# Moving the steps of a weight folding within the first image's attention, and converting five more score tiles by DMA

## The chip, the cores and the metric

The kernel runs on one core of a Trainium2 chip. A core has a matrix engine (TensorE, PE in the profile), a vector engine (VectorE, DVE), a scalar engine (ScalarE, ACT), a general engine (GpSimd, POOL) and an engine that mostly issues DMAs (SyncE, SP). Each engine works through its own list of instructions in order, and engines wait for each other through semaphores. The metric is the device time of one execution in microseconds (us), as the median of several runs. Lower is better.

## The reference, cut to what matters

Two layers are applied to a tensor of 8 images, 512 channels and 32 x 32 pixels. Each is a normalisation, an attention over the 1024 pixels and a projection with a residual. The first has 8 heads of 64 channels and rounds q, k and v to 8 bits; the second has one head of 512 channels.

```
# layer 0
h = group_norm(x)
q, k, v = split(qkv_w @ h + qkv_b)            # 8 heads of 64 channels
q, k, v = fake_quant(q), fake_quant(k), fake_quant(v)
w = softmax(q*s . k*s)                        # over 1024 keys
x = x + proj_w @ (w . v) + proj_b
# layer 1
t = group_norm(x)
q, k, v = t @ wq.T + bq, t @ wk.T + bk, t @ wv.T + bv
x = x + (softmax(q . k / sqrt(512)) . v) @ wp.T + bp
```

For layer 1 the kernel needs only two products of weights, wq with wk and wv with wp. It forms them once. This is the folding, whose steps the change moves.

## The kernel before

The kernel has three stages: q, k and v of all images, with the ranges for the rounding; the first image's attention in layer 0; then, for each image, its projection and layer 1, into which the attention of the next image is woven.

**Units of attention.** The attention of layer 0 is cut into units, numbered by u through all images. A unit is one pair of heads (j), one half of the 1024 queries (hf) and one of eight blocks of 128 keys (s). So u % 8 is s, and an image has 64 units: units 0 to 63 are the first image's, and unit 64 is the second's first. For each unit:

- `scores(u)` forms both heads' scores on PE in a PSUM tile st, and ACT writes their exponential (exp) as 32-bit floats. There are two such PSUM tiles. The scores of unit u + 2 wait until the exponential of unit u has been taken.
- `split(u)` turns the exponential (pt) into two 16-bit parts in the tile two: a copy of it in float16, and what the copy lost, which DVE subtracts (`rest`). Who makes the copy depends on the image and on s. In the first image a DMA issued by GpSimd makes it for s in `CAST_BY_DMA` (0, 1, 4), DVE for s = 6, and ACT for s = 2 and 5. Units with s = 3 and 7 are used as 32-bit floats (the tile aside), without a copy. In later images there are no such plain units: GpSimd copies s = 2 and 6, DVE copies s = 5 while the order is still the first image's, and ACT copies the others. A copy by DMA reads from one of three slots in a buffer called spare, not from a pt tile, and its subtraction is put off (`put_off`) to the third split after it or to when the parts are needed.
- `over_keys` multiplies the parts with v (av), and `totals` sums them (sm), both on PE, two units at a time. After the eighth key block `finish` has ACT copy av and sm out (to ao, and to rs or kept_u). The sums go through DRAM to be inverted and spread (`spread`), and DVE multiplies (`divide`).

In the loop the scores run six to nine units ahead of over_keys.

**Pairs.** `load_pair` loads the raw q, k and v of the next pair through SP's queue, and DVE rounds them (raw, q, k, v). In the first image's order these small works, with `spread` and `divide`, stand in a list `dealt`. Each call of split takes one that is due.

**Folding.** `fold()` is a generator. Each `next` carries out one step up to the next yield. For each of two products there are 16 steps of one 128x512 product on PE (fold), and every fourth is followed by an ACT copy (to wa or wm). A step with wt_f multiplies a widened vector that DVE must have written (into the first part of spare, from four reductions called z); ACT copies its result to fold_room. The next step, wc_f, multiplies fold_room by a constant. After the first product the generator also puts four additions (wa) in the list dealt and issues the loads of the projection weights and of the first image's input (`load_x2`, tile h, two DMAs of 1 MB). That input takes the place of the weights that wt_f reads last. At its end it puts four additions (wm) and two kinds of stores in the list. In all there are 35 yields. Nine steps are taken before the attention starts, the others inside `scores`, where the chosen units take one ahead of their products. Whatever is left runs when the first image's last unit is done.

**Order.** A helper class `InOrder` records the order of the instructions of PE, DVE and ACT (line 91 for DVE and ACT, line 209 for PE in the profile). While the first image's attention is recorded, its order is as written. Afterwards a planner with estimated costs orders the work of the later images. Its clock is set to PE's when planning begins, after two more groups of four units (`LEAD = 2`), so units up to 77 are scored and split in the order as written.

The lines that decide about the steps and the copies:

```
CAST_BY_DMA, CAST_BY_DVE = (0, 1, 4), (6,)
...
                if u % 8 in (1, 4, 6):
                    next(folding, None)
...
                elif b == 0 and s in CAST_BY_DMA:
                    at = (u // NT * len(CAST_BY_DMA) + CAST_BY_DMA.index(s)) % 3
...
                if b == 0 and s in CAST_BY_DMA:
                    nc.gpsimd.dma_start(two[:, 0], pt)
                    put_off[u] = rest
                    return
```

Of the kernel before, what the change touches and what calls it, by code (L numbers as in the profile page):

```python
# [22 lines left out]
NT = T // P  # L23
NH = T // 512
HEADS = 8
PAIRS = HEADS // 2
# [32 lines left out]
def attn_pair_kernel(  # L59
# [12 lines left out]
    class InOrder:  # L72
# [74 lines left out]
        def settle(self, what):  # L147

            while True:
                i = next((i for i, c in enumerate(self.chores) if c[0] == what), None)  # L150
                if i is None:
                    return
                self.begin(i)
# [3 lines left out]
    def elements(n):  # L157

        return 0.21 + n * 0.957e-3
# [4 lines left out]
    def awaits(t):  # L164

        pe.t = max(pe.t, t + 0.1)
# [41 lines left out]
    def mm(ps, lhsT, rhs, **kw):  # L208
        ins = nc.tensor.matmul(ps, lhsT=lhsT, rhs=rhs, **kw).ins  # L209
        part = lhsT.shape[-1] / P if lhsT.shape[-1] in (32, 64) else 1.0  # L210
        if rhs.dtype in (BF, F16, F32R):
            part *= 0.25 * lhsT.shape[0] / P
        pe.t += math.prod(rhs.shape[1:]) * 1.677e-3 * part
        if last_mm[0] is not None:
            tc.add_manual_dep(ins, last_mm[0].name, IN_ORDER, reason="order")
        last_mm[0] = ins
# [90 lines left out]
    with ExitStack() as fast:  # L307
        wts = fast.enter_context(tc.tile_pool(name="wts", bufs=1))
        def pair_ps(name):
            return ps_s.tile([P, 2, 512], F32, tag="s", name=name)  # L310
# [602 lines left out]
        def plain(b, s):  # L913
            return b == 0 and s % 4 == 3
# [4 lines left out]
        def deal(u):  # L919
            i = next((i for i, (at, *_) in enumerate(dealt) if at <= u), None)  # L920
            if i is not None:
                dealt.pop(i)[2]()
                if dealt[i : i + 1] and dealt[i][2].__name__ == "fetch_v":
                    dealt.pop(i)[2]()
# [7 lines left out]
            dve.settle(what)  # L932

        ao = {}
        CAST_BY_DMA, CAST_BY_DVE = (0, 1, 4), (6,)

        def load_pair(b, j, u=None):

# [54 lines left out]
        def attention():  # L993
# [13 lines left out]
            def scores(u):  # L1007
                b, j, hf, s = units[u]
                if hf == 0 and s == 0:
                    settle("qk")  # L1010
                nm = f"{b}_{j}_{hf}"
                qt, kt, _ = pairs[b, j]
                st = pair_ps(f"st_{nm}_{s}")
                if u % 8 in (1, 4, 6):
                    next(folding, None)
                awaits(st_free[-2])
                for i, r in enumerate(HALF):
                    mm(
                        st[:, i, :], lhsT=kt[r, bass.ts(s, P)],
                        rhs=qt[r, bass.ts(hf, 512)], start=True, stop=True,  # L1020
                    )
                if u >= 4:
                    need(u - 4)
                if plain(b, s):
                    pt = aside[:, u // 4 % 3].rearrange("p (i k) n -> p i (k n)", i=2)
                elif b == 0 and s in CAST_BY_DMA:
                    at = (u // NT * len(CAST_BY_DMA) + CAST_BY_DMA.index(s)) % 3
                    pt = spare[:, 1 + 2 * at : 3 + 2 * at].rearrange("p i k n -> p i (k n)")
                else:
                    pt = ptp.tile([P, 2, 512], F32, tag="p", name=f"pt_{nm}_{s}")  # L1030
                there = act.do(
                    1.12, lambda: act.activation(pt, st, AF.Exp, scale=esc),
                    max(pe.t + 0.25, ready.get(u - 4, 0.0) + 0.1),
                )
                st_free.append(there)
                pts[u] = pt, there

            def split(u):

                b, j, hf, s = units[u]  # L1040
                pt, there = pts.pop(u)
                if not InOrder.planned:
                    for v in [v for v in put_off if v < u - 2]:
                        put_off.pop(v)()
                    deal(u)
                if plain(b, s):
                    parts[u], ready[u] = pt, there
                    return
                two = partp.tile([P, 2, 2, 512], F16, tag="two", name=f"two_{b}_{j}_{hf}_{s}")
                parts[u] = two  # L1050

                def rest():
                    dve.tensor_tensor(two[:, 1], pt, two[:, 0], ALU.subtract)
                    ready[u] = dve.t

                if b == 0 and s in CAST_BY_DMA:
                    nc.gpsimd.dma_start(two[:, 0], pt)
                    put_off[u] = rest
                    return

                def cast(copy=act.copy):
                    at_hand.add(u)
                    copy(two[:, 0], pt)  # L1063
                    done_at = act.t if copy == act.copy else there + 1.5
                    dve.later("sum", elements(1024), rest, done_at + 0.1, 9.0)

                if b == 0:
                    cast(dve.tensor_copy if s in CAST_BY_DVE else act.copy)
                elif s % 4 == 2:
                    cast(nc.gpsimd.tensor_copy)  # L1070
                elif not InOrder.planned and s == 5:
                    cast(dve.tensor_copy)
                else:
                    act.later("cast", 1.02, cast, there, 7.0)

            def need(u):

                if u in put_off:
                    put_off.pop(u)()
                while u not in ready:  # L1080
                    e, name = (act, "cast") if u not in at_hand else (dve, "sum")
                    e.begin(next(i for i, c in enumerate(e.chores) if c[0] == name))
# [95 lines left out]
            for u in (0, 2, 4):  # L1178
                for i in (u, u + 1):
                    scores(i)  # L1180
                    split(i)
                yield 0
            for u in range(0, len(units), 4):
                b, j, hf, s = units[u]
# [15 lines left out]
                if not late:  # L1200
                    two(scores, u + 6)
                if late:
                    over_keys((u, u + 1))
                    two(scores, u + 6)
                    totals((u, u + 1))
                    over_keys((u + 2, u + 3))
                    totals((u + 2, u + 3))
                    two(split, u + 6)
                    two(scores, u + 8)
                elif dense:  # L1210
                    over_keys((u, u + 1))
                    totals((u, u + 1))
                    two(split, u + 6)
                    two(scores, u + 8)
                    over_keys((u + 2, u + 3))
                    totals((u + 2, u + 3))
                else:
                    over_keys(range(u, u + 4))
                    totals(range(u, u + 4))
                    two(split, u + 6)  # L1220
                    two(scores, u + 8)
# [1011 lines left out]
```

## Time and profile before

| | us |
|---|---|
| median of 3 runs | 2589.24 (2586.92 to 2589.48) |
| the profiled execution | 2589.42 |
| its span, first to last instruction | 2587.6 |

| Engine | busy us | share of the span |
|---|---|---|
| PE | 2524.7 | 98% |
| DVE | 1896.7 | 73% |
| ACT | 1352.1 | 52% |
| POOL | 183.7 | 7% |

The shares are means over the stages. In the stretch that the change touches ACT and DVE are far busier than over the whole:

| Stretch, us | length | PE | DVE | ACT | DMA share |
|---|---|---|---|---|---|
| 586 to 600 | 14 | 10.41 | 9.64 | 12.76 | 0.58 |
| 600 to 616 | 16 | 16.00 | 15.03 | 14.40 | 0.57 |
| 616 to 640 | 24 | 21.63 | 17.41 | 19.12 | 0.86 |
| 640 to 664 | 24 | 23.62 | 23.28 | 22.13 | 0.50 |
| 664 to 690 | 26 | 25.54 | 21.88 | 23.57 | 0.73 |
| 690 to 716 | 26 | 21.40 | 23.36 | 25.45 | 0.32 |

A matmul's end is modelled in the profile, so that a PE that reads as full may still be waiting in small gaps. In the lines of the profile an entry begins with its start and duration in us, then the engine, the line, the operation, and what is written from what. The number in square brackets is how long the engine was idle before it, and what ended that. A "x2" at the end of an entry means that two such instructions were merged.

### The profile page before, as it was taken

To read this page: it belongs to the slowest core of one execution; us is meant where nothing else is said; L and a number is where in the kernel's file an instruction comes from. 1 tells how busy PE (TensorE), PEld (TensorE's weight loads), DVE (VectorE), ACT (ScalarE), POOL (GpSimd) and SP (SyncE) were. 2 spreads that over 40 slices of the span, in tenths; PEclk is the share of its full clock that TensorE was granted. 3 is DMA by queue.
4 is the path that set the end of the run, shared out by engine and by line. 5 is a ranking of instruction groups with operands and counts; after the bars stand their busy time and mean duration, and the time that the engine had idled before them with its cause. 6 is when DMAs were issued, how large, how long until landed. Compare 5 with 4: busy or idle time off the path is not lost.

```text
span 2587.6 us, 38715 instructions
## 1 busy us (share of the span) xinstructions
PE 2524.7 (98%) x15670; PEld 1748.4 (68%) x15670; DVE 1896.7 (73%) x2748; ACT 1352.1 (52%) x1688; POOL 183.7 (7%) x161
## 2 busy tenths in 40 slices
PE   7999999999979999999999999999999999999998
PEld 4788888872237766775677577657756775777787
DVE  6788777658867777777877787777777777775544
ACT  3222222218946665665666466747665665664121
POOL 0000000001100001000100010010001000100000
PEclk9999999999989999999999999999999999999999
DMA  4343333337521232223212321232232123212211
GB/s 167 134 150 135 119 117 117 128 127 183 138 85 46 73 112 90 62 78 115 86 55 86 113 94 58 95 118 65 73 111 94 46 79 123 85 52 82 86 38 39
DMA packets 159469, 249.38 MB, mean 96 GB/s; under 512 B 26928, under 2 KB 93488, under 8 KB 157744
## 3 DMA queue, kind: packets, MB, share of 16 engines
q1 hardware_dynamic: 125264, 182.81, 21.3%
q10 hardware_dynamic: 30560, 57.71, 6.6%
q0 software_dynamic: 3456, 6.29, 1.3%
q8 instruction: 125, 2.05, 0.3%
q14 instruction: 64, 0.52, 0.1%
HBM read 153.64 MB, written 86.28 MB: 93 GB/s over the span
## 4 chain that ended last, share of the span: by engine, by line
PE 85%; DVE 4%; issue 3%; ACT 2%; DMA 1%; POOL 0%; SPq 0%; ACTq 0%; DVEq 0%; POOLq 0%
PE s L209 15%; PE o L209 14%; PE qkps L209 12%; PE pj L209 8%; PE av L209 8%; PE v2ps L209 7%; PE g L209 7%; PE vps L209 6%; PE st L209 4%; PE sm L209 3%; DVE two L91 1%; ACT pt L91 1%; DMA two<-spare 1%; DVE acc L91 1%; DVE h L91 0%
## 5 line engine op out<-in xcount | busy, mean ns | idle before, releaser
L91 ACT ACTIVATE pt<-st,esc 128x1024 f32<-128x1024 f32 x472 | 501.9, 1114 | 345.0 <-PE st L209 330.4
L91 DVE TENSOR_TENSOR two<-pt,two 128x1024 f16<-128x1024 f32 x472 | 567.1, 1215 | 141.1 <-POOL two L1063 104.7
L91 ACT CAST two<-pt 128x1024 f16<-128x1024 f32 x350 | 354.7, 1055 | 13.0 <-PE sm L209 7.7
L209 PE MATMUL av<-two,v 128*32 128x512 f16 x3968 | 247.1, 382 | 12.7 <-DVE v L91 9.0
L1063 POOL CAST two<-pt 128x1024 f16<-128x1024 f32 x112 | 148.1, 1322 | 1451.6 <-PE sm L209 774.5
L209 PE MATMUL s<-g,h 128*128 128x256 f32 x1024 | 233.4, 380 | 0.0
L209 PE MATMUL pj<-ao,wp 128*128 128x512 f32 x512 | 224.9, 597 | 0.7 <-DVE h L91 0.4
L209 PEld LDWEIGHTS s<-g,h 128*128 128x128 f32 x1024 | 193.0, 190 | 30.9 <-issue 4.3
L209 PEld LDWEIGHTS <-v 128*32 128x32 f16 x3968 | 91.5, 96 | 152.6 <-issue 69.4
L91 ACT ACTIVATE u_ring<-qkps,qkbt 128x512 f32<-128x512 f32 x89 | 61.2, 687 | 252.3 <-PE qkps L209 237.5
L209 PEld LDWEIGHTS pj<-ao,wp 128*128 128x128 f32 x512 | 96.3, 191 | 123.5 <-issue 111.6
L209 PE MATMUL s<-g,sums 128*128 128x256 f32 x768 | 178.4, 381 | 0.2 <-DVE p L91 0.2
L209 PE MATMUL st<-q,k 64*128 64x512 bf16 x1024 | 162.8, 383 | 14.0 <-ACT pt L91 8.0
L209 PE MATMUL o<-p,v 128*128 128x256 f32 x768 | 175.2, 382 | 0.9 <-DVE p L91 0.9
L209 PEld LDWEIGHTS o<-p,v 128*128 128x128 f32 x768 | 144.3, 190 | 27.1 <-issue 5.7
L209 PEld LDWEIGHTS s<-g,sums 128*128 128x128 f32 x768 | 144.6, 190 | 24.2 <-issue 3.7
L209 PE MATMUL sm<-two,ones 128*32 128x512 f16 x1984 | 137.1, 381 | 0.0
L209 PE MATMUL qkps<-half,w_high 128*128 128x512 f32 x480 | 134.2, 402 | 0.0
L209 PE MATMUL qkps<-half,w_low 128*128 128x512 f32 x480 | 131.7, 397 | 2.3 <-DVE half L91 2.3
L209 PE MATMUL qkps<-half,w_mix 128*128 128x512 f32 x480 | 131.0, 395 | 1.1 <-DVE half L91 1.1
L209 PEld LDWEIGHTS <-k 64*128 64x128 bf16 x1024 | 33.9, 94 | 140.6 <-issue 137.8
L209 PE MATMUL g<-h,wa 128*128 128x256 f32 x512 | 120.7, 384 | 0.0
(224 smaller groups left out, 3890.6 us busy)
## 6 DMA issues: line engine op xcount, KB each, us to landing
rs<-rs_d SPq DMA_DIRECT2D x76, 256.0 KB
x<-in_x_dram SPq DMA_DIRECT2D x32, 512.0 KB
q_d<-wa SPq DMA_DIRECT2D x32, 512.0 KB
k_d<-wa SPq DMA_DIRECT2D x32, 512.0 KB
v_d<-v_ring SPq DMA_DIRECT2D x32, 512.0 KB
raw<-q_d SPq DMA_DIRECT2D x32, 512.0 KB
raw<-k_d SPq DMA_DIRECT2D x32, 512.0 KB
x_d<-h SPq DMA_DIRECT2D x64, 256.0 KB
```

Source lines behind the costliest of these rows:

```text
L91: ins = self.latest = op(*args, **kw).ins
L209: ins = nc.tensor.matmul(ps, lhsT=lhsT, rhs=rhs, **kw).ins
L1063: copy(two[:, 0], pt)
```

## The change

The steps of the folding are taken ahead of other units: ahead of each of the first ten units (before: units 1, 4, 6 and 9 of them), ahead of units with u % 8 = 1 or 5 in between (before: 1, 4 or 6), and ahead of each unit from 60 on (`FEW`). The 26 yields that are left when the attention starts, and the end of the generator, are used up at unit 64. And the condition for a copy by DMA no longer asks for the first image but for a unit below 74 (`BY_DMA`), so units 64, 65, 68, 72 and 73 of the second image are copied by a GpSimd DMA, from the slots in spare, and not by ACT. Their subtractions on DVE are put off like those of the first image.

```diff
-        CAST_BY_DMA, CAST_BY_DVE = (0, 1, 4), (6,)
+        CAST_BY_DMA, CAST_BY_DVE, BY_DMA, FEW = (0, 1, 4), (6,), PAIRS * NH * NT + 10, PAIRS * NH * NT - 4
...
                 st = pair_ps(f"st_{nm}_{s}")
-                if u % 8 in (1, 4, 6):
+                if u < 10 or u % 8 in (1, 5) or u >= FEW:
                     next(folding, None)
                 awaits(st_free[-2])
...
-                elif b == 0 and s in CAST_BY_DMA:
+                elif u < BY_DMA and s in CAST_BY_DMA:
                     at = (u // NT * len(CAST_BY_DMA) + CAST_BY_DMA.index(s)) % 3
                     pt = spare[:, 1 + 2 * at : 3 + 2 * at].rearrange("p i k n -> p i (k n)")
...
-                if b == 0 and s in CAST_BY_DMA:
+                if u < BY_DMA and s in CAST_BY_DMA:
                     nc.gpsimd.dma_start(two[:, 0], pt)
                     put_off[u] = rest
                     return
```

PAIRS is 4, NH is 2 and NT is 8, so the two constants are 74 and 60.

## The prediction

> **What bounds the kernel now.** I read the page first (shares, chain), then stretches of 8 us, then the order of time where they have holes. The chain of waits:
>
> ```profile
> PE 85%; DVE 4%; issue 3%; ACT 2%; DMA 1%; POOL 0%; SPq 0%; ACTq 0%; DVEq 0%; POOLq 0%
> ```
>
> TensorE (PE) sets most of the kernel, but the change touches only the first image's attention, 64 units from about 588 us to 705 us, and what follows to 733 us. Stretches there (length, then busy PE, weight loads, DVE, ACT, POOL; clock; DMA share):
>
> ```profile
> 592.00:600.00 8.00, 5.57 (x40) 1.66 (x38) 5.87 (x11) 7.94 (x10) 0.55 (x2) 1.00 0.53 97
> 600.00:608.00 8.00, 8.00 (x86) 2.39 (x84) 7.89 (x10) 7.09 (x8) 1.59 (x3) 1.00 0.60 135
> 624.00:632.00 8.00, 5.79 (x55) 2.03 (x54) 5.38 (x11) 5.84 (x6) 1.06 (x2) 0.96 0.86 208
> 632.00:640.00 8.00, 8.00 (x64) 1.91 (x63) 6.97 (x8) 5.28 (x7) 0.53 (x1) 0.82 0.82 208
> 696.00:704.00 8.00, 7.27 (x84) 2.76 (x75) 5.46 (x6) 7.97 (x11) 2.46 (x1) 1.00 0.19 66
> 704.00:712.00 8.00, 4.75 (x58) 1.76 (x58) 7.93 (x11) 7.97 (x9) 1.43 (x2) 1.00 0.18 69
> ```
>
> Here PE, ACT and DVE are all near full. PE has two holes: the start, and 624 to 632. At the end (696 to 712) ACT is full and PE waits for it. The second hole, in order of time:
>
> ```profile
> 617.79 0.95 SPq L1235 DMA_DIRECT2D h<-in_x_dram  x2
> 620.13 0.53 POOL L1057 DMA_DIRECT2D two<-spare  x1 [4.59 <-ACT spare L91]
> 629.09 1.23 DVE L91 TENSOR_TENSOR two<-spare,two 128x1024 f16<-128x1024 f32 x1 [2.55 <-DMA two<-spare]
> 634.27 1.11 ACT L91 ACTIVATE spare<-st,esc 128x1024 f32<-128x1024 f32 x1 [3.64 <-PE st L209]
> ```
>
> The 2 MB load of h goes out, the converting DMA of unit 20 follows, lands 8.9 us later (median 3.7), and DVE, PE and ACT stand. The cycle of eight units from unit 26's exp to unit 34's takes 16.35 us (627.58 to 643.93); its neighbours take 12.3 to 13.1. That stall costs some 4 us. How image 1's projection starts:
>
> ```profile
> 717.84 1.27 DVE L91 SCALAR_TENSOR_TENSOR ao<-ao,scl,kept_u 128x1024 f32<-128x1024 f32 x1
> 719.17 4.56 PE L209 MATMUL pj<-ao,wp 128*128 128x512 f32 x10 [0.31 <-DVE ao L91]
> 723.35 0.74 DVE L91 SCALAR_TENSOR_TENSOR h<-pj,vec,h 128x512 f32<-128x512 f32 x1
> 724.15 7.13 PE L209 MATMUL pj<-ao,wp 128*128 128x512 f32 x16 [0.42 <-DVE h L91]
> ```
>
> From 703.5 to 724 the chain is DVE: PE waits for its division (ao) and first eviction (h).
>
> **What the Trainium skill says.** "DMA: Bandwidth & Descriptors", section "SWDGE vs HWDGE vs iDMA": a converting DMA must come from GpSimd, and its queue shares each DMA engine in turn with the plain loads. The trace agrees: latencies of 2.8 us in quiet stretches, 8.9 us beside the load of h. "TensorE: Matmul & The Clock Gate", Part 1: a PE idle for a window of about 3.4 us falls to half clock. The trace shows a granted 0.82 after the second hole. "SBUF — State Buffer", "SBUF: two separate sides": DVE copies can keep GpSimd from writing descriptors. The trace can't separate this from queueing.
>
> **The start: ten folding steps where four were.** One step is one 128x512 fp32 product, two records: 1.06 us from its start to the next score (588.22 to 589.28). Units 0 to 9 now take steps 10 to 19 of the generator: six more, two of them special. Step 17 (wt_f, 0.96 us, 616.69 to 617.65) and step 18 (wc_f, 0.99 us) were at units 20 and 22; now they are at 7 and 8. Walking the orders: unit 0's scores come 1.06 us later, but exp 0 only about 0.4 (ACT's table load ends at 589.03). Exps 2 to 6 run 1.15 us late, partly from a second fold copy of 0.59 us. Step 17 must wait for DVE's widened weights (four writes of spare, ended 599.1 before, some 599.4 now). ACT must copy wt_f's result (0.58 us) ahead of exp 7, since ACT is in order, and step 18 waits for that copy. I get exp 7 at 601.1 (598.74 before), exp 8 at 603.5 (599.74) and exp 9 near 604.9 (601). Six steps are 6.4 us of PE; the holes at the start take about 2.5. Cost: **+3.9 us**, bounds +2.5 and +5.
>
> **The middle: 12 steps for 18 in units 10 to 59.** Six steps fewer are 6.4 us of PE, but most of it was covered. ACT's work for eight units is 8 exps at 1.0 us from start to start, two casts at 0.96, two evictions at 0.59 and half a fold copy: 11.4 us of a 12.4 us cycle. What stops ACT is the wait for the third score of each eight (0.56 to 0.83 us; 0.83 at 656.39 and 669.29). That comes from the step ahead of the second score, which stays. With the change I reckon a cycle of 12.1: the two at 12.9 and 13.1 gain 0.8 each, others 0.2 or 0.3, less DVE's new load early. DVE's chores of the folding (4 wa at 0.66, 4 reductions at 0.72, the widening 0.7) move to units 8 to 26, where DVE's own 20.3 us of work becomes 24.4 in about 25. Gain: **-1.2 us**, bounds 0 and -2.7.
>
> **The load of h moves.** It stands behind wt_f, so it leaves at some 600.6 instead of 617.8. The old stall goes: **-4.0 us**. What is late next: the DMAs of units 8 and 9, issued near 604.7 and 606.1 behind that load and two raw loads of 0.5 MB each. At about 270 GB/s (what 618 to 629 shows) the load alone is done near 608. DVE wants unit 8 at 611. A 3.7 us latency costs nothing; 8.9 us costs 2.6 us on DVE and then PE. I take **+2.0 us**, bounds 0 and +3.7.
>
> **The end.** Units 60 to 63 take four steps instead of two, and the last (wc_f) stands ahead of unit 64 instead of 70. The same work, earlier: exp 62 about 1.75 us later. Five casts of image 2 (units 64, 65, 68, 72, 73) leave ACT: 5 x 1.0 us of the 24.1 us from exp 62 to exp 76. They become five GpSimd DMAs of 0.53 us each, and GpSimd, idle for 5 us or more between casts, hides these. ACT is then no longer the limit. But the subtractions stay on DVE (1.15 us each in a row), and the chain was on DVE from 703.5. From unit 61's subtraction to the first eviction DVE takes 33.7 us before (689.64 to 723.35), 3 us of it idle. After, the same list gains two quantising steps of pair 1 (raw 0.66, k 0.75), starts 1.1 us later, and by my addition ends at 723 to 724.5. In addition SP's order has a 512 KB load of v between the store of the reciprocals and the read back into kept_u. That read took 6.4 us from store to division (711.42 to 717.84) and will take some 8, so PE, with the last units earlier, waits for ao longer: its second projection tile ends about 1 us later than 723.7, plus some half clock. Gain -0.3 from k (0.35 us wait at 733.58). Net: **+1.0 us**, bounds -2 and +3. Everything past 735 us stands in the same order on all queues and shifts whole.
>
> **The sum.** +3.9 - 1.2 - 4.0 + 2.0 + 1.0 = +1.7 us on the profiled 2589.42 (span 2587.6), that is 2591.1. The median of the runs is 2589.24, 0.2 us below; I say 2591.
>
> **Rivals.** I call 0.2% (5.2 us) what a measurement of this kernel can tell from no change.
>
> No measurable change (48%): the sum above, between 2586 and 2594.
>
> Slower (34%): the load of h strikes again, at units 8 and 9. For: both converting DMAs are in its shadow at a time when DVE has no slack, since it holds the moved chores. Price: the stall's 4 us returns in full (+2 over my value) and DVE's lag of 1 to 2 us is kept; with the start that makes +5.5 to +9, 2595 to 2598. It decides once the latency of unit 8's DMA passes about 6.5 us. Against: it leaves 4 us after the load, where unit 20's left 2.3.
>
> Faster (18%): the middle is PE's after all. PE reads 7.6 to 8.0 of 8 us there; if all six steps come back (-6.4 instead of -1.2), and the load hides, +3.9 - 6.4 - 4.0 - 1 = -7.5, 2582. Against: DVE and ACT are each over 90% there, and the end is DVE's.
>
> That the casts do not move is excluded: the order shows five more DMAs on GpSimd, five casts fewer on ACT.
>
> **Numbers.** Faster 0.18, same 0.48, slower 0.34. The likeliest case's own range is 2586 to 2594; leaving a tenth on each side gives 2583 to 2598.
>
> **What would show it.** Exp 9 near 605 (start); no DVE wait above 2 us for a converting DMA near 620 to 630 (stall gone), and the landing of units 8 and 9 under 6.5 us; cycles of 12.1 us from unit 18 on; ACT with holes from 697 us while DVE is full to the first eviction, at 723 to 725. If exp 58 stands more than 3 us ahead of 682.35, the middle is mis-sized; if the eviction comes before 720, the DVE bound at the end is wrong.

## The result and the profile after

The changed kernel takes 2597.65 us, the median of 10 runs (2596.34 to 2601.3), beside 2589.92 us for the kernel before on the same chip. The ratio is 1.0031, with a 95% interval of 1.0023 to 1.0040: some 7.7 us slower. Its profiled execution took 2598.39 us, with a span of 2596.6 us (before: 2587.6).

The chain of waits of the changed kernel says nothing new. TensorE carries the same share:

```profile
PE 85%; DVE 4%; ACT 2%; issue 2%; DMA 1%; POOL 0%; SPq 0%; ACTq 0%; DVEq 0%; POOLq 0%
```

So the time must be looked for by stretches. These are of the changed kernel (start and end in us, length, then busy PE, weight loads, DVE, ACT, POOL, each with its number of instructions; granted clock; DMA share; GB/s):

```profile
600.00:608.00 8.00, 8.00 (x90) 3.23 (x88) 6.09 (x9) 5.20 (x6) 1.30 (x2) 1.00 0.86 286
608.00:616.00 8.00, 5.87 (x54) 1.64 (x51) 3.77 (x4) 7.71 (x9) 0.53 (x1) 1.00 0.84 208
616.00:624.00 8.00, 7.53 (x66) 2.10 (x65) 7.93 (x11) 3.67 (x5) 1.53 (x2) 0.79 0.35 66
704.00:712.00 8.00, 4.94 (x62) 1.71 (x61) 7.97 (x9) 7.24 (x9) 2.95 (x3) 1.00 0.64 188
712.00:720.00 8.00, 7.35 (x54) 2.47 (x53) 7.96 (x11) 5.56 (x7) 1.20 (x1) 0.79 0.57 131
720.00:728.00 8.00, 3.69 (x5) 1.51 (x5) 6.83 (x7) 0.00 (x0) 0.00 (x0) 0.72 0.42 113
728.00:736.00 8.00, 8.00 (x17) 3.49 (x16) 2.83 (x5) 0.00 (x0) 0.00 (x0) 0.85 0.17 66
```

There are two holes. In the first, 608 to 624, DVE falls to 3.77 of 8 us, then ACT to 3.67, and the clock to 0.79. It is the hole that the kernel before had near 624 to 640, moved forward. The second, 720 to 736, is new: PE does 3.69 of 8 us, and when PE works again the clock is below one. (ACT does nothing there, but it stands in the kernel before too, 13.49 us up to 731.65: it waits for PE's next scores.)

The first hole in order of time, from the timelines of SP, POOL, DVE and ACT:

```profile
600.26 0.94 SPq L1235 DMA_DIRECT2D h<-in_x_dram  x2
604.72 0.77 POOL L1057 DMA_DIRECT2D two<-spare  x1 [7.68 <-ACT spare L91]
604.74 0.57 SPq L949 DMA_DIRECT2D raw<-v_d  x1
606.10 0.53 POOL L1057 DMA_DIRECT2D two<-spare  x1 [0.61 <-ACT spare L91]
606.19 0.33 SPq L949 DMA_DIRECT2D raw<-q_d  x1
610.85 1.22 DVE L91 TENSOR_TENSOR two<-spare,two 128x1024 f16<-128x1024 f32 x1
615.19 1.23 DVE L91 TENSOR_TENSOR two<-spare,two 128x1024 f16<-128x1024 f32 x1 [2.52 <-DMA two<-spare]
```

The copies of units 8 and 9 go out at 604.72 and 606.10. Unit 8's is there when DVE wants it, unit 9's lands 9.1 us after its issue (615.19 less 606.10), and DVE stands 2.52 us.

The second hole, in the same way:

```profile
714.32 1.00 DVE L91 TENSOR_TENSOR rcs<-apart 128x16 f32<-128x16 f32 x1
715.63 0.32 SPq L1163 DMA_DIRECT2D rs_d<-rcs  x1
716.21 0.58 SPq L949 DMA_DIRECT2D raw<-v_d  x1
717.04 1.13 SPq L1165 DMA_DIRECT2D kept_u<-rs_d  x2
717.37 2.84 PE L209 MATMUL pj<-ao,wp 128*128 128x512 f32 x6
723.19 1.29 DVE L91 SCALAR_TENSOR_TENSOR ao<-ao,scl,kept_u 128x1024 f32<-128x1024 f32 x1 [1.14 <-DMA kept_u<-rs_d]
724.53 14.31 PE L209 MATMUL pj<-ao,wp 128*128 128x512 f32 x26 [4.32 <-DVE ao L91]
727.39 0.74 DVE L91 SCALAR_TENSOR_TENSOR h<-pj,vec,h 128x512 f32<-128x512 f32 x1
738.76 0.61 PE L209 MATMUL st<-q,k 64*128 64x512 bf16 x4
```

The same steps in the kernel before:

```profile
710.94 0.17 DVE L91 TENSOR_TENSOR rcs<-apart 128x16 f32<-128x16 f32 x1
711.42 0.32 SPq L1163 DMA_DIRECT2D rs_d<-rcs  x1
712.89 1.16 SPq L1165 DMA_DIRECT2D kept_u<-rs_d  x2
```

The sums for the reciprocals (rcs) are added 3.4 us later than before, the 512 KB load of v is issued between the store and the read back, the division comes at 723.19 (before: 717.84), and PE stands 4.32 us after six matmul records of the projection. Then its 26 other records take 14.31 us, where the kernel before took 4.56 and 7.13 us for them with small waits. The first score after that stands at 738.76, before at 731.22.

Here are the places again in one table, each counted from exp 0 of its own profiled execution, because exp 0 itself stands anywhere between 586.0 and 590.7 us from one execution to the next (where the timeline merges two exponentials, the second is put 1.0 us after the first). "Score" is the first score after the projection's first half.

| Kernel | exp 10 | exp 18 | exp 26 | exp 34 | exp 58 | exp 64 | ao | score |
|---|---|---|---|---|---|---|---|---|
| before | 13.81 | 26.23 | 38.53 | 54.88 | 93.30 | 102.46 | 128.79 | 142.17 |
| after | 17.53 | 33.48 | 45.76 | 58.27 | 95.03 | 107.30 | 134.09 | 149.66 |
| difference | +3.72 | +7.25 | +7.23 | +3.39 | +1.73 | +4.84 | +5.30 | +7.49 |

Read along the last row: the start adds 3.7 us, units 8 and 9 add 3.5, the old stall's absence takes 3.8 off, the cycles to exp 58 take 1.7 off, and from there to the score 5.8 are added. The two spans differ by 9.0 us, so 1.5 more come after the score in these two executions. That part was not taken apart.

### The profile page after: what moved, and what is told of

It is laid out like the page before. It is cut to its first block, busy times and chain, and to the rows that moved or that the text cites. A ratio compares the mean times of both kernels' runs of the same rounds, so it can differ in the third digit from the quotient of the medians.

```text
span 2596.6 us, 38715 instructions
## 1 busy us (share of the span) xinstructions
PE 2529.5 (97%) x15670; PEld 1752.4 (67%) x15670; DVE 1898.9 (73%) x2748; ACT 1346.5 (52%) x1683; POOL 186.8 (7%) x166
## 4 chain that ended last, share of the span: by engine, by line
PE 85%; DVE 4%; ACT 2%; issue 2%; DMA 1%; POOL 0%; SPq 0%; ACTq 0%; DVEq 0%; POOLq 0%
PE s L209 15%; PE o L209 14%; PE qkps L209 12%; PE pj L209 9%; PE av L209 8%; PE v2ps L209 7%; PE g L209 6%; PE vps L209 6%; PE st L209 4%; PE sm L209 3%; DVE two L91 1%; ACT pt L91 1%; PE fold L209 1%; DVE h L91 0%; DVE acc L91 0%
## 5 line engine op out<-in xcount | busy, mean ns | idle before, releaser
L91 ACT ACTIVATE pt<-st,esc 128x1024 f32<-128x1024 f32 x467 | 496.2, 1114 | 353.6 <-PE st L209 339.2
```

Of the source, the lines that this page charges most:

```text
L91: ins = self.latest = op(*args, **kw).ins
```

## The experiments

The theory at the outset: the load of h strikes at units 8 and 9, and the end loses because ao is late, since the moved steps put other work of DVE, and the load of v, ahead of the way from the sums to ao. The rivals: the five copies by DMA make the loss at the end; or the end is full in any case and takes back whatever is won ahead of it. A measured time is a median, with its ratio to the kernel before and the interval of that; before took 2589.1 to 2589.3 us beside these runs.

### Steps and copies apart

The steps as changed, image 2's copies at ACT again:

```diff
-                elif u < BY_DMA and s in CAST_BY_DMA:
+                elif b == 0 and s in CAST_BY_DMA:
...
-                if u < BY_DMA and s in CAST_BY_DMA:
+                if b == 0 and s in CAST_BY_DMA:
```

> The changed kernel with the five units of image 2 copied by ACT again, as before the change; the folding steps stay where the change put them. Theory (the end loses because the wm additions and two quantising steps now stand ahead of the sums' reciprocals on DVE, so that ao is late): most of the loss stays without the copies by DMA, exp 58 at +1.8 us against before, the reciprocals (rcs) at least 2.5 us late, 2593 to 2596 us. Rival (the five copies by DMA make the loss at the end, by themselves): the end adds nothing to the +1.8, 2591 to 2592 us.

Measured: 2596.5 us, 1.0030 (1.0019 to 1.0041). And the reverse, the copies alone in the kernel before:

```diff
-                elif b == 0 and s in CAST_BY_DMA:
+                elif u < PAIRS * NH * NT + 10 and s in CAST_BY_DMA:
...
-                if b == 0 and s in CAST_BY_DMA:
+                if u < PAIRS * NH * NT + 10 and s in CAST_BY_DMA:
```

> The kernel before with only the copies by DMA up to unit 73; all folding steps stand where they stood before. Theory: the wm additions come no earlier than before, so the reciprocals (rcs) stay within 1 us of 710.94 and the first projection waits for ao by less than 2 us: 2588 to 2591 us, no measurable change. Rival (the copies by DMA themselves make the loss at the end): +3.5 to +5 us, 2593 to 2595 us.

Measured: 2591.05 us, 1.0004 (0.9995 to 1.0012), no difference. So the steps carry the loss (more of it than I expected, the whole) and the copies as such carry none. What the first run expected of exp 58 and of rcs stays open: its profiled execution took 2601.77 us, 5.3 above its median, and is not read here. But the copies bring nothing either, and the trace of the copies alone says why. The projection in it, from PE's timeline:

```profile
711.22 2.84 PE L209 MATMUL pj<-ao,wp 128*128 128x512 f32 x6
719.23 13.12 PE L209 MATMUL pj<-ao,wp 128*128 128x512 f32 x26 [5.17 <-DVE ao L91]
```

With ACT relieved, PE is at the projection 3.7 us earlier than before, counted from exp 0 (122.56 to 126.26). It then waits 5.17 us for an ao that is no earlier (division at 717.89, before 717.84), and runs the 26 records in 13.1 us. I had expected a wait under 2 us: the time was right, the wait was not.

### The load of h in pieces

The 2 MB load is cut into eight of 256 KB. GpSimd issues each behind a copy by DMA (of units with s = 1 or 4), so that its own order paces them:

```diff
-        ao = {}
+        ao, pieces = {}, []
...
-                    load_x2(0, nc.sync.dma_start)
+                    load_x2(
+                        0, lambda t, src: pieces.extend(
+                            (t[:, cc], src[:, cc]) for cc in range(CC)
+                        ),
+                    )
...
-                    nc.gpsimd.dma_start(two[:, 0], pt)
+                    copy = nc.gpsimd.dma_start(two[:, 0], pt)
+                    if pieces and s:
+                        piece = nc.gpsimd.dma_start(*pieces.pop(0))
+                        tc.add_manual_dep(piece.ins, copy.ins.name, IN_ORDER, reason="order")
```

In the changed kernel:

> The changed kernel, but the 2 MB load of h is cut into eight pieces of 256 KB, each issued by GpSimd behind a copy by DMA of units 9 to 36 instead of all at once by SP near 600 us. Theory (the load of h stalls units 8 and 9): the cycle from exp 10 to exp 18 falls from 15.95 us to 12.3 to 12.8, no copy by DMA takes over 6 us to land, and the kernel takes 2593 to 2595 us. Rival (the stall of 3.7 us is made good later, in the DVE-bound end): the cycle falls but the kernel stays at 2596.5 to 2598 us.

Measured: 2594.98 us, 1.0024 (1.0014 to 1.0034), as expected, though this interval and the changed kernel's overlap. The cycle from exp 10 to exp 18 falls from 15.95 to 13.03 us, but unit 9's copy still takes 7.8 us, not under 6 as expected (from POOL's and DVE's timelines):

```profile
603.71 0.53 POOL L1057 DMA_DIRECT2D two<-spare  x1 [0.61 <-ACT spare L91]
611.49 1.23 DVE L91 TENSOR_TENSOR two<-spare,two 128x1024 f16<-128x1024 f32 x1 [1.20 <-DMA two<-spare]
```

Two loads of 512 KB (v and q of the next pair) go out beside the copies here, at 602.35 and 603.80, as in the changed kernel, and the first piece of h right behind unit 9's copy (604.37). In the kernel before they went out at 604.69 and 606.14, after the copies of units 8 and 9 (601.16 and 602.33). The ten steps at the start have pushed these copies into the loads. From exp 10 to exp 26 the kernel before takes 24.72 us, the changed one 28.23, this one 26.33. So of the 3.5 us at units 8 and 9 about 1.9 are the load of h as a whole; 1.6 stay without it. (Four other kernels with the changed kernel's order up to there took 27.54 to 29.45 us.)

In the kernel before:

> The kernel before with the load of h cut into the same eight pieces, behind the copies by DMA of units 25 to 52. Theory: the cycle from exp 26 to exp 34 falls from 16.35 us to 12.3 to 13, and the kernel takes 2585 to 2587 us. Rival (the time comes back at the end): 2588.5 to 2590 us.

Measured: 2585.78 us, 0.9988 (0.9980 to 0.9996), inside what was expected. The exponentials of units 26 and 34 in it, from ACT's timeline, now 12.34 us apart and no longer 16.35:

```profile
627.79 1.12 ACT L91 ACTIVATE pt<-st,esc 128x1024 f32<-128x1024 f32 x1 [0.79 <-PE st L209]
640.13 1.11 ACT L91 ACTIVATE pt<-st,esc 128x1024 f32<-128x1024 f32 x1 [0.56 <-PE st L209]
```

The old stall was the load of h, and its 3 us do reach the end. The pieces go out not only smaller but also later (627.96 to 671.74 us, before 617.79); no run separates the two.

### The end: which limit

First the last pair's reciprocals and division alone, moved ahead in the list of dealt works; all else as in the changed kernel:

```diff
+                    elif j == PAIRS - 1:
+                        dealt.insert(0, (u + 14, "ao", divide))
                     else:
                         dealt.append((u + 20, "ao", divide))
...
+                elif j == PAIRS - 1:
+                    dealt.insert(0, (u + 10, "ao", spread))
                 else:
                     dealt.append((u + 12, "ao", spread))
```

> The changed kernel, but for the first image's last pair the reciprocals of the sums are taken at split 70 and ahead of whatever else is due (instead of split 72 in its turn), and the division (ao) at split 74 (instead of after split 77). Nothing else moves. Theory (the end's loss is the late ao): rcs near 709.6 us instead of 714.32, PE waits for ao by less than 1 us instead of 4.32, the projection runs at full clock, then waits for its first evictions; 3.5 to 5 us are gained, 2592.5 to 2594.5 us. Rival (the end is late because the units themselves are late and DVE is full): ao comes earlier but the first score after the projection does not, 2596.5 to 2598 us.

Measured: 2597.19 us, 1.0032 (1.0022 to 1.0043). The theory as I had put it falls: ao came 5.1 us earlier (129.00 us after exp 0), PE did not wait for it, and no gain was measured. The trace, from DVE's and PE's timelines:

```profile
717.81 1.28 DVE L91 SCALAR_TENSOR_TENSOR ao<-ao,scl,kept_u 128x1024 f32<-128x1024 f32 x1 [2.54 <-DMA kept_u<-rs_d]
718.63 7.20 PE L209 MATMUL pj<-ao,wp 128*128 128x512 f32 x16
727.87 0.75 DVE L91 SCALAR_TENSOR_TENSOR h<-pj,vec,h 128x512 f32<-128x512 f32 x1
728.67 8.83 PE L209 MATMUL pj<-ao,wp 128*128 128x512 f32 x16 [2.84 <-DVE h L91]
```

The first eviction is no earlier than in the changed kernel (727.39), and PE, after two PSUM tiles, waits for it. But DVE stood 2.54 us idle for the read of kept_u: the trial had put the division ahead of its data, and so lengthened the very list that now bounds. That gave a new theory: two limits lie within a microsecond of each other, ao, and DVE's list up to the first eviction; a cure must shorten both. The next trial has the division one split later (`u + 15`):

> The changed kernel with the last pair's reciprocals at split 70 and its division at split 75: one split later than in the trial with split 74, where DVE stood 2.54 us for the read of kept_u. Theory (two limits end within a microsecond of each other at the projection: ao, and DVE's list up to the first eviction; the trial at 74 took the first away and lengthened the second): DVE waits less than 0.5 us, the first eviction stands 2 to 2.5 us earlier than in the changed kernel counted from its first exp, PE waits for ao by less than 0.5 us: 2594 to 2595.5 us. Rival (the end is set by how late the units are, whatever DVE does with ao): 2596.5 to 2598 us.

Measured: 2593.28 us, 1.0016 (1.0010 to 1.0023). From the timelines of SP, DVE and PE:

```profile
707.17 0.32 SPq L1163 DMA_DIRECT2D rs_d<-rcs  x1
709.70 1.14 SPq L1165 DMA_DIRECT2D kept_u<-rs_d  x2
712.62 0.56 SPq L949 DMA_DIRECT2D raw<-v_d  x1
715.45 1.27 DVE L91 SCALAR_TENSOR_TENSOR ao<-ao,scl,kept_u 128x1024 f32<-128x1024 f32 x1
716.78 4.56 PE L209 MATMUL pj<-ao,wp 128*128 128x512 f32 x10 [1.39 <-DVE ao L91]
722.57 0.74 DVE L91 SCALAR_TENSOR_TENSOR h<-pj,vec,h 128x512 f32<-128x512 f32 x1
723.37 8.83 PE L209 MATMUL pj<-ao,wp 128*128 128x512 f32 x16 [2.03 <-DVE h L91]
```

The read back now goes out ahead of the load of v, DVE does not wait at the division, and the first eviction is 2.0 us earlier than in the changed kernel counted from exp 0 (136.31 to 138.29). PE's wait for ao was 1.39 us, not under 0.5 as expected. The score comes 3.8 us earlier, of which 0.7 is there at exp 58 already, where the two kernels have the same order. The loss beside the kernel before falls from 7.7 to 4.0 us. From exp 58 to the score this kernel takes 51.5 us, the changed one 54.6, the kernel before 48.9: moving two small works in an order gave back 3.1 of the end's 5.8 us.

Then the last units without their steps:

```diff
-                if u < 10 or u % 8 in (1, 5) or u >= FEW:
+                if u < 10 or u % 8 in (1, 5):
```

> The changed kernel without the steps ahead of each unit from 60 on: units 61, 65 and 69 take one, the last comes after the first image's last unit, and the wm additions come after it. Theory: only two of the four wm additions stand ahead of the reciprocals, and the 512 KB load of v stands behind the read back into kept_u, so that ao comes 3 to 4.5 us earlier than in the changed kernel; 2592 to 2594.5 us. Rival (the steps at the end are harmless, the loss is from the start and the copies by DMA): 2596 to 2598 us.

Measured: 2593.43 us, 1.0016 (1.0009 to 1.0023). The loss beside the kernel before falls to 4.3 us. exp 64 stands 3.1 us earlier than in the changed kernel, ao 3.0, the score 3.5. So the steps ahead of units 60 to 64 also make the units themselves late, and that reaches the score. From exp 58 to the score this gives back 3.4 of the 5.8 us. These and the 3.1 of the reordering are not to be added, since both shorten the same way to ao. With either alone some 2.5 us of the end stay; the combined kernel below has both, beside other changes, and takes 45.6 us from exp 58 to the score.

### The start alone

```diff
-                if u % 8 in (1, 4, 6):
+                if u < 10 or u % 8 in (1, 4, 6):
```

> The kernel before with only the ten steps ahead of the first ten units; the others stand ahead of units with u % 8 = 1, 4 or 6 as before, so that the generator is used up near unit 52 and the last units have none. Theory (the start costs what it adds, +3.7 us, and the load of h strikes at units 8 and 9 in full): exp 18 stands 7 us later than before, exp 34 3 to 3.7 us later, and the end with fewer steps gives back 0 to 2 us: 2591 to 2594.5 us. Rival (the same steps only change places, so what the start adds the end gives back in full): 2588 to 2590.5 us.

Measured: 2596.64 us, 1.0029 (1.0018 to 1.0039), above what either theory gave. exp 10 stands at +3.7 as expected, but a further stall came between exp 34 and exp 42 (16.80 us for the cycle). From the timelines of SP, POOL and DVE:

```profile
636.06 0.59 SPq L949 DMA_DIRECT2D raw<-v_d  x1
636.94 1.16 SPq L1165 DMA_DIRECT2D rs<-rs_d  x2
638.19 0.54 SPq L1799 DMA_DIRECT2D wm_d<-wm  x1
638.74 0.53 POOL L1057 DMA_DIRECT2D two<-spare  x1 [4.86 <-ACT spare L91]
648.22 1.23 DVE L91 TENSOR_TENSOR two<-spare,two 128x1024 f16<-128x1024 f32 x1 [3.69 <-DMA two<-spare]
```

No load of h is near. Three other bulk transfers stand ahead of the copy, and it takes 9.5 us. From rcs to the division it takes 10.22 us, before 6.90, so 3.3 us are lost there too. To separate the start from the load of h, the same kernel with the load in pieces:

> The kernel before with the load of h in eight pieces and the ten steps ahead of the first ten units (units from 10 on take steps ahead of u % 8 = 1, 4 or 6 as before, until none is left near unit 52). Against the kernel with the pieces alone (2585.8 us) only the start differs, and the steps missing later. Theory (the start costs 3.7 us of its own and little of it comes back): exp 10 at +3.7 us, 2588.5 to 2590.5 us. Rival (what the start adds comes back from the later units, where PE was the limit): 2585 to 2587 us.

Measured: 2593.64 us, 1.0014 (1.0007 to 1.0021), against 2585.78 for the pieces alone: +7.9 us, again more than expected. In the two profiled executions the lead of the kernel with pieces alone is 3.4 us at exp 10, 5.6 at exp 34, 2.9 at exp 64, and 2.7 at the reciprocals. So the start's 3.4 us grow to 5.6, and 2.7 of these come back between exp 34 and exp 64, where this kernel takes fewer steps. What is left there does not make 7.9. At ao the lead is 6.2: another 3.5 us come between the reciprocals and ao (SP's, DVE's and PE's timelines):

```profile
711.02 0.32 SPq L1166 DMA_DIRECT2D rs_d<-rcs  x1
713.54 0.57 SPq L949 DMA_DIRECT2D raw<-v_d  x1
714.22 1.24 SPq L1168 DMA_DIRECT2D kept_u<-rs_d  x2
720.93 1.28 DVE L91 SCALAR_TENSOR_TENSOR ao<-ao,scl,kept_u 128x1024 f32<-128x1024 f32 x1 [2.70 <-DMA kept_u<-rs_d]
722.27 13.58 PE L209 MATMUL pj<-ao,wp 128*128 128x512 f32 x26 [4.85 <-DVE ao L91]
```

From rcs to the division it takes 10.39 us, with the pieces alone 6.90. The folding's steps end early here, so do the works they put in the list; the quantising of the next pair is then dealt sooner (q at 711.99, with the pieces alone at 717.86), and the load of v stands ahead of the read into kept_u in SP's list. It waits there for this quantising, so that the read goes out 3.20 us after the store, with the pieces alone 1.45. The kernel before is spared by its order: there the load of v comes after that read, at 721.60.

### Versions that beat both

The first of these has the steps of the kernel before, the load of h in pieces, the five copies by DMA, the reciprocals at split 70, the division at 74, and the copies of units 69 and 77 at ACT (two lines of `split` taken out):

```diff
-                elif not InOrder.planned and s == 5:
-                    cast(dve.tensor_copy)
```

> The folding steps of the kernel before, with the load of h in eight pieces, image 2's five copies by DMA, the last pair's reciprocals at split 70 and division at split 74, and the copies of units 69 and 77 made by ACT instead of DVE. Theory: the stall of the load of h goes (some -3), and, since ACT no longer limits the end and ao is no longer late, the first score after the projection's first half stands 5 to 7 us earlier than before: 2582 to 2584.5 us. Rival (DVE's list up to the first eviction bounds the end whatever its order): 2585.5 to 2587 us, no better than the pieces alone.

Measured: 2585.32 us, 0.9986 (0.9979 to 0.9993). That is no better than the pieces alone, nearer to the rival; DVE stood 3.07 us for kept_u, as in the first trial of the order. With the division at split 75:

> The combined kernel (steps as before the change, h in pieces, five copies by DMA, reciprocals at split 70, units 69 and 77 copied by ACT) with the division at split 75 instead of 74, where DVE stood 3.07 us for kept_u. Theory: the first eviction comes 2 to 3 us earlier, and the kernel takes 2582 to 2583.5 us. Rival (PE arrives early, idles, and pays in granted clock what it won): 2585 to 2586 us.

Measured: 2579.57 us, 0.9965 (0.9953 to 0.9977), 9.7 us below the kernel before, below what was expected, and with the next one below every other kernel tried. From PE's timeline:

```profile
705.86 2.84 PE L209 MATMUL pj<-ao,wp 128*128 128x512 f32 x6
709.70 4.56 PE L209 MATMUL pj<-ao,wp 128*128 128x512 f32 x10 [0.99 <-DVE ao L91]
715.56 7.13 PE L209 MATMUL pj<-ao,wp 128*128 128x512 f32 x16 [1.30 <-DVE h L91]
722.63 0.60 PE L209 MATMUL st<-q,k 64*128 64x512 bf16 x4
```

Two short waits, and no slow matmul. Counted from exp 0 the score stands 6.2 us earlier than before. Some more is won later: a wait of PE for DVE's v of 8.95 us at 764.72 in the kernel before has no counterpart here, where no wait of PE between 735 and 785 us is above 2.42 us. That was seen, and not taken apart. Nor does a run have the order and the pieces without the five copies, so what the copies add here is not shown.

Last, the change's thinner middle added to this:

```diff
-                if u % 8 in (1, 4, 6):
+                if u % 8 in ((1, 4, 6) if u < 42 else (1, 5)):
```

> The same combined kernel, with the folding steps ahead of units with u % 8 = 1 or 5 from unit 42 on (1, 4 or 6 up to there); the last three steps come after the first image's last unit, ahead of unit 70. Theory (the change's middle is worth what its cycles say, 12.2 us against 12.9 and 13.1 in the two cycles from unit 42 to 58): exp 58 stands 1 to 1.5 us earlier counted from exp 0, and of that 0 to 1.5 us reach the end, 2581 to 2583.5 us. Rival (the end is DVE's and takes it back): as the combined kernel with split 75, within 0.5 us.

Measured: 2581.01 us, 0.9968 (0.9956 to 0.9980), not different from the one without it (2579.57), and at the lower edge of what the theory gave; the rival is not ruled out. exp 58 stands 1.1 us earlier, as expected; the score stands 2.1 us later, since the last steps run ahead of unit 70. What the middle gives, the end takes in this trace.

## Why the prediction was right or wrong

The direction and size that I held likeliest, no measurable change at 2591 us, did not come: it is 0.31% slower. The time lies inside the wide range of 2583 to 2598 us, but by a third of a microsecond, and with the end mis-sized by 4.8 us that is luck. The rival "slower" gave 2595 to 2598 us and holds the time, but its mechanism, the stall at units 8 and 9, is only a part of it. Its sum does not come out of its terms either: 1.7 us, 2 more for the stall and 1 to 2 for DVE's lag are 4.7 to 5.7 us, not 5.5 to 9. By the prediction's own steps:

- **The start** (+3.9): measured +3.72 at exp 10. exp 8 was put at 603.5 and stands at 603.31, exp 9 at 604.9 and stands at 604.69. Right. How much of it comes back later no run shows by itself: with the pieces, 2.9 us of lead are left at exp 64, after 5.6 at exp 34.
- **The middle** (-1.2): -1.7, that is -1.66 from exp 34 to 58 and nothing between 18 and 26. The cycles from exp 18 on are 12.2 to 12.5 us, beside 12.1 predicted. The mechanism was right, the size close.
- **The old stall** (-4.0): -3.84. Right, and the run with pieces in the kernel before shows that the load of h was its cause.
- **The new stall** (+2.0): +3.5, near the end of its bounds. The mis-sized term: I priced the load of h alone, and held that it would be done near 608. The two 512 KB loads with which units 8 and 9 now coincide were named and not priced; in the run with pieces some 1.6 us are left with them and one piece of h. And I took unit 8's copy as the one that decides; it landed in 5.65 us and cost nothing, and unit 9's, 9.07 us, decided.
- **The end** (+1.0): +5.8 from exp 58 to the score. This is the step that failed. Counted from exp 0, the changed kernel is 1.7 us late at exp 58, 2.9 where DVE's list starts, 4.2 at the store of the reciprocals, 5.3 at ao and 7.5 at the score. I took DVE's list as one sum from unit 61's subtraction up to the first eviction, and put it at 32.3 to 33.8 us (33.7 before). It took 34.8, with 1.14 of waiting for kept_u, and it started 2.9 us late, not 1.1. Its start before and after:

```profile
689.64 1.23 DVE L91 TENSOR_TENSOR two<-pt,two 128x1024 f16<-128x1024 f32 x1
692.59 1.23 DVE L91 TENSOR_TENSOR two<-pt,two 128x1024 f16<-128x1024 f32 x1 [1.21 <-ACT two L91]
```

And what decides is an item inside the list, the reciprocals. I lengthened the way from their store to the division (to some 8 us; it took 7.6, before 6.4) and gave no lateness to the store itself. It went out 4.2 us later: 2.9 from the start of the list, 0.4 from the list (all four additions of wm and a quantising step now stand ahead of the reciprocals, before two additions), and 0.8 from the addition of rcs, which took 1.00 us instead of 0.17. So ao came at 723.19, and PE waited 4.32 us for it. The first eviction, put at 723 to 724.5, came at 727.39. PE's second tile did not end "about 1 us later" than 723.7: its eviction stands at 732.01, after a wait of 3.15 us for PE. And "some half clock" was 2.6 us: 26 records in 14.31 us, beside 4.56 and 7.13 in the kernel before. Two runs bear this out, each with more than half of the 5.8 us given back: the reciprocals taken first, and the last units without their steps.

The five copies were expected to take the limit of the end from ACT, and did: with the copies alone PE is at the projection 3.7 us earlier. That they then give nothing, alone or with the steps, is shown by the pair of runs that take them apart.

The slow addition of rcs is a cost that the prediction did not have. A copy by GpSimd was under way at it (714.09 to 715.29). In all five kernels where that addition begins during such a copy (1.00 or 1.01 us in three, 0.25 and 0.35 in two) it ends within 0.03 us of the copy's end; in the nine others it takes 0.16 or 0.17 us. The Trainium skill ("SBUF — State Buffer", section "SBUF: two separate sides") says that a DVE instruction with two inputs in SBUF and a GpSimd instruction that reads SBUF share one pair of ports as an exclusive lock, so that one of them stands until the other's instruction is over. The traces agree. But this doesn't make DVE's list longer than before as a whole: the kernel before pays as much at other places (1.52 instead of 0.69 us for its copy at 704.70, 1.52 instead of 0.68 for an addition of wm at 712.39). It matters in the changed kernel because it falls on the way to ao.

## What to carry to other kernels

When works are moved in an engine's list, don't only add up the list: find the one item whose result goes on a long round trip (here reciprocals to DRAM and back, 6.9 to 10.4 us from the addition of rcs to the division), see what the new order puts ahead of it on its engine and on the DMA queue, and issue it first, but take its result no earlier than it lands. A bulk load beside small transfers on the critical path can be cut up and paced by the engine that issues the small ones; here that gave 3.3 us. And relieving an engine need not give time: with ACT relieved alone, PE only waited longer for ao.

## What the hardware showed that was not expected

- A copy of 256 KB that converts takes 8.9 to 9.1 us beside 2 MB and 1 MB of plain loads (unit 9's, in six kernels), 9.5 us beside a load of 512 KB, a spreading read and a store, and still 7.8 us beside two loads of 512 KB and a piece of 256 KB; in quiet stretches it took 2.8 us. The Trainium skill ("DMA: Bandwidth & Descriptors", section "Queues, rings and completion order") says that each DMA engine goes round the queues that have work, a packet at a time. The traces agree in so far as the copy, though on a queue of its own, is slowed by others' loads. The same section says that on each DMA engine descriptors are consumed in ring order, though a later one may finish its write first; the slower read into kept_u behind the load of v, on SP's queue, fits that.
- PE can pay for a wait after it. With waits of 4.3 to 5.2 us ahead of them the same 26 records took 13.12 us (copies alone), 13.58 (start and pieces) and 14.31 us (changed kernel), and 4.56 and 7.13 us, 11.7 together, with waits of 0.99 and 1.30 us (combined kernel). "TensorE: Matmul & The Clock Gate", Part 1, of the Trainium skill names an idle window of about 3.4 us. But waits of 1.39 and 2.03 us, 4.56 us of work apart, were enough in the trial with split 75, where the 16 records after the second took 8.83 instead of 7.13 us, and one wait of 1.96 us in the kernel before with the pieces, where the 26 records took 13.12 us. After a wait of 3.03 us in the run of the start alone they took only 11.43 us. So in these runs the length of the wait just ahead does not tell the cost.
- The size of a stall varies between executions of nearly the same order: from exp 10 to exp 18 the changed kernel takes 15.95 us, and 14.25 us in the trial with split 75, which differs from it only some 90 us later.
